# Attention over 32 steps on one core: rows' exponentials kept in every second step, exchanged in one pass

## The chip, the core and the metric

The kernel runs on one core of a Trainium2 chip. A core has a matmul engine (TensorE, PE in the profile, with its weight loads as PEld), VectorE (DVE), ScalarE (ACT), GpSimd (POOL), a queue engine that issues transfers (SyncE, SP) and 16 DMA engines. PE writes its results into PSUM, eight banks of 512 fp32 values on each of 128 partitions; everything else is in SBUF. The engines run beside one another and wait for each other on semaphores; each takes its own instructions in order. The metric is the device time of one execution in microseconds (us).

## The reference

```python
# x: (8, 512, 512) f32, cond: (8, 512); 16 heads of 32
Q, K, V   = split_heads(x @ Wq.T + bq), split_heads(x @ Wk.T + bk), split_heads(x @ Wv.T + bv)
tQ, tK    = split_heads(tokens @ Wq.T + bq), split_heads(tokens @ Wk.T + bk)   # tokens = cond[:, None, :]
scores    = einsum('bhqd,bhkd->bhqk', Q + tQ, K + tK) / sqrt(32)
attn      = softmax(scores, axis=-1)
out       = x + merge_heads(einsum('bhqk,bhkd->bhqd', attn, V))
```

All in fp32. There are 8 batches of 512 rows, and 16 heads.

## The kernel before, in words

The work is cut into T = 32 steps. Step t treats batch b = t // 4 and four heads (group g = t % 4), each head on 32 partitions or columns of a tile of 128.

A step needs, for each head, the scores with the queries on the partitions ("row scores", `row_scores`, L585: four blocks qc of 128 queries against 512 keys). VectorE takes their maxima (`one_max`, L552, or two heads at once in `row_max_of`, L594), ScalarE their exponentials with the row sums (`denominators`, L640). For the product with V, PE wants the exponentials with the keys on the partitions. There are two ways to get them.

In an ordinary step PE makes the scores a second time, transposed (`exponentials`): L692 puts the negated maximum into the bank, split into three bf16 parts, and L695 adds the scores; ScalarE writes the exponentials as tiles "e" (L706). The first exponentials are thrown away after their sums. The maxima reach L692 by `split_max` (four small operations, L654 to L657) and `turn_max` (a transposing DMA, L666).

In a step of the list `BLOCKED` (L71: 3, 7, ... 27, seven steps) the first exponentials are kept: `denominators` writes them to an SBUF tile of 32 KB a partition, VectorE transposes them in blocks of 32 x 32 (`turn_blocks`, L605, 8 units of 1024 columns), and SP's transfers exchange the blocks between the four groups of 32 partitions (`swap_blocks`, L624): for each half of the rows six pairs are swapped by three moves through two tiles from the pool of "e", 36 transfers of 128 KB a step. No second scores, maxima's split or transposes are made for such a step. `times_v` (L715) reads either kind.

Projections of x to Q, K and V are made for two groups of a batch at a time with seven products instead of eight (`product`, L441). `first_products` combines them on VectorE, `first_by_others` has ScalarE copy them and GpSimd add them, `other_products` does the second half on VectorE. `combine_x` and `combine_w` prepare sums of blocks on GpSimd.

The main loop (L1009) runs t from 1 to 28 with four items each. Every item has one row of scores (of step t + 1, the last one of step t + 2) and one piece of PE work: "q", "k" or "v" (a projection product for a later batch) or "V" (`weighted`: the product of step t − 1 with V, the sums spread by `spread_sums`, the reciprocal, and `send`). In a step that isn't kept, an item also makes a quarter of the step's second scores. `send` transposes the result on VectorE (L779), scales it and adds the residual x on GpSimd (L780, L781) and stores it with SP. `load_residual` (L188, L196) loads x and adds the bias on GpSimd. `turn_x` (L351) transposes the next batches' x on VectorE, and `load_block` (L170) loads it with SP. The eight PSUM banks are handed from item to item by `begin` and `released`.

The order of PE, ScalarE, VectorE and GpSimd is the order of the program text; SP's transfers are ordered by the scheduler. After the loop, steps 29 to 31 are finished by code of their own, with the tile "late" in the room of the kept rows.

Of the kernel before, what the change touches and what calls it, by code (L numbers as in the profile page):

```python
# [17 lines left out]
def kernel(  # L18
# [52 lines left out]
    BLOCKED = [t for t in range(3, T - 4, G)]  # L71
# [3 lines left out]
    xp = ctx.enter_context(tc.tile_pool(name="xp", bufs=3))  # L75
    xtp = ctx.enter_context(tc.tile_pool(name="xtp", bufs=2))
    qkp = ctx.enter_context(tc.tile_pool(name="qkp", bufs=3))
    ep = ctx.enter_context(tc.tile_pool(name="ep", bufs=10))
# [100 lines left out]
    def load_residual(t):  # L179

        b, g = divmod(t, G)
        if turned_by_vector(t):
            if late:
                xr[t] = late[0][:, 2, :].rearrange("p (f e) -> p f e", e=BL)
            else:
                xr[t] = op.tile([P, NB, BL], F32, tag="xr", name=f"xr_{t}")
            for h in range(HG):
                nc.sync.dma_start(  # L188
                    xr[t][h * BL : (h + 1) * BL], spread(x[b], g * P + h * BL)
                )  # L190
            bias = bvs[:, g, :].unsqueeze(1).broadcast_to([P, NB, BL])
        else:

            xr[t] = xT[b][:, g, :]
            bias = bvl.broadcast_to([P, S])
        nc.gpsimd.tensor_tensor(xr[t], xr[t], bias, ALU.add)  # L196

    EB = ctx.enter_context(tc.tile_pool(name="eb", bufs=1))

    def room(name):  # L200
        return EB.tile([P, HG, NS, HG, P], F32, tag="eb", name=name)

    early = room("early").rearrange("p g c h s -> p (g c) (h s)")
# [4 lines left out]
    def load_w(n, w, queue, cs=range(NC)):  # L208
        wv = w.rearrange("(c p) d -> p c d", p=P)
        for c in cs:  # L210
# [9 lines left out]
                mybir.EngineType.Pool,  # L220
            }
# [108 lines left out]
    def transpose_x(n, pt, leaves=nc.vector.tensor_copy):  # L330

        b, sc = divmod(n, NS)
        if b >= B:
            return
        if sc == 0:
            xT[b] = xtp.tile([P, NC, S], F32, tag="xT", name=f"xT_{b}")
        for cc in range(NC):
            nc.tensor.transpose(
                pt[:, cc * P : (cc + 1) * P], xs[n][:, cc * P : (cc + 1) * P], ident
            )  # L340
        leaves(xT[b][:, :, sc * P : (sc + 1) * P], pt.rearrange("p (c s) -> p c s", c=NC))
        if n:
            load_block(n + 3)

    def turn_x(n):
        b, cc = divmod(n, NC)
        if b >= B:
            return
        if cc == 0:
            xT[b] = xtp.tile([P, NC, S], F32, tag="xT", name=f"xT_{b}")  # L350
        nc.vector.transpose(xT[b][:, cc, :], xs[n].rearrange("p f i -> p (f i)"))  # L351
        to_load.append(n + 3)
# [136 lines left out]
    def first_by_others(n, b, u, dens, small, at):  # L489

        one_, two_ = banks(at), banks(at + 1)
        c1, c12, c2, c22 = parts_of(n, b, u)
        dens()
        product(n, b, u, 1, one_[:, :HS])
        product(n, b, u, 6, two_[:, HS:])
        small()
        product(n, b, u, 2, two_[:, :HS], (0,))
        product(n, b, u, 7, one_[:, HS:])
        m1 = c2[:, 0, :]
        nc.scalar.copy(m1, one_[:, :HS])  # L500
        if n == "v":
            nc.scalar.copy(c1[:, 0, :], two_[:, :HS])
            nc.scalar.copy(c12, two_[:, HS:])
            nc.scalar.copy(c22, one_[:, HS:])
        else:
            nc.scalar.copy(c1, halves(two_))
            add = tok[:, "qk".index(n), u * 2 + 1, b : b + 1]
            nc.scalar.activation(c22, one_[:, HS:], AF.Identity, bias=add)
        for o in (c1[:, 0, :], c12):
            nc.gpsimd.tensor_tensor(o, o, m1, ALU.add)  # L510
        nc.gpsimd.tensor_tensor(c22, c22, c12, ALU.add)
# [44 lines left out]
    def row_max(t, qc, hold=False, w=HG):  # L556
# [14 lines left out]
        def held():  # L571
            if apart or hold and t < T - 2:
                for j in range(2):
                    one_max(t, qc, 2 + j, last[j])
            else:
                row_max_of(t, qc, 1, both)
# [21 lines left out]
    blocked = {}  # L598

    def turn_blocks(t, units):  # L600

        for n in units:
            pr = slice(n % NP * 2, n % NP * 2 + 2)
            e = blocked[t][:, :, n // NP, pr, :].rearrange("p g h s -> p g (h s)")
            nc.vector.transpose(e, e)  # L605

    APART = [(a, g) for a in range(HG) for g in range(a + 1, HG)]
    between = {}

    def swap_blocks(t, half, move):  # L610

        def part(a, g):
            e = blocked[t][a * BL : (a + 1) * BL, g, half * 2 : half * 2 + 2]
            return e.rearrange("p c h s -> p (c h s)")

        if move == 0:
            between[t, half] = [
                ep.tile([P, 2, S], F32, tag="e", name=f"between_{t}_{half}_{i}") for i in range(2)
            ]
        for n, (a, g) in enumerate(APART):  # L620
            at = (n + 2) % HG * BL
            kept = between[t, half][n // HG][at : at + BL].rearrange("p i s -> p (i s)")
            to, of = [(kept, part(a, g)), (part(a, g), part(g, a)), (part(g, a), kept)][move]
            nc.sync.dma_start(to, of)  # L624

    def denominators(t, qc, w=HG):
# [3 lines left out]
        for j in range(HG):  # L630
            if t in BLOCKED:
                if t not in blocked:
                    blocked[t] = room(f"blocks_{t}")
                to = blocked[t][:, :, qc, j, :].rearrange("p g (c e) -> p g c e", e=BL)
            else:
                to = banks(w + j)
# [50 lines left out]
    def exponentials(t, kc, at=None):  # L687
# [5 lines left out]
        for j in range(HG):  # L693
# [7 lines left out]
            )  # L701
        for pr in range(NP):
            e = ep.tile([P, 2, S], F32, tag="e", name=f"e_{t}_{kc}_{pr}")
            es[t, kc, pr] = e
# [3 lines left out]
    def times_v(t, kc, pt, chunks=range(NS)):  # L708
        b, g = divmod(t, G)
        for j in range(HG):  # L710
            if t in BLOCKED:
                e = blocked[t][:, :, :, j, kc * BL : (kc + 1) * BL].rearrange("p a c e -> p c a e")
# [63 lines left out]
    def send(t, y_, rec):  # L776

        y = op.tile([P, NB, BL], F32, tag="res", name=f"res_{t}")
# [3 lines left out]
        b, g = divmod(t, G)  # L782
        for h in range(HG):
            nc.sync.dma_start(spread(out[b], g * P + h * BL), y[h * BL : (h + 1) * BL])  # L784
# [167 lines left out]
    load_residual(1)  # L952
# [19 lines left out]
    def products(t, n, blocks, hold, dens, small):  # L972

        b, r = (t - 1) // G + 1, (t - 1) % G
        if r % 2:
            hold()
            other_products(n, b, r // 2, dens, small, (0, 3))
            released(1, 2, 4, 5, 6, 7, 0, 3)
        elif blocks and n == "v":
            first_products(n, b, r // 2, dens, small, 5, 4, hold)  # L980
            released(6, 7, 0, 1, 2, 3, 5, 4)
        elif blocks:
            hold()
            first_by_others(n, b, r // 2, dens, small, 4)
            released(6, 7, 0, 1, 2, 3, 5, 4)
        else:
            first_products(n, b, r // 2, dens, small, 1, 0, hold)
            released(2, 3, 4, 5, 6, 7, 1, 0)

    TURNED = [((1, 1), (0, 1), (0, 1), (0, 1)), ((0, 0), (0, 1), (0, 1), (0, 1))]  # L990
    turned = {}

    def turn_more(t, i, late):

        for u in (t, t + 1):
            if u in BLOCKED:
                n = turned.get(u, 0)
                turned[u] = n + TURNED[t + 1 - u][i][late]
                turn_blocks(u, range(n, turned[u]))

    SWAPS = {
        (-1, 2): [(0, 0)],
        (-1, 3): [(0, 1), (0, 2)],
        (0, 3): [(1, 0)],
        (1, 0): [(1, 1)],
        (1, 1): [(1, 2)],
    }

    for t in range(1, T - 3):  # L1009
# [3 lines left out]
        items = ["q", "k", "v", "V"] if t - 1 in BLOCKED else ["V", "q", "k", "v"]  # L1013
        for i, item in enumerate(items):
# [4 lines left out]
            late_first = item in ("v" if blocks else "qkv") and t % 2 == 1  # L1019
            hold = row_max(*rows, late_first, w)  # L1020

            def held(i=i, hold=hold):
                hold()
                if i == 2:
                    split_max(t + 1)
                    turn_max(t + 1)

            dens = lambda: denominators(*rows, w)
            if item in "qkv":
                products(t, item, blocks, held, dens, nothing)  # L1030
            else:
                held()
                dens()
                if blocks:
                    weighted(t - 1, banks(4), banks(5), nothing)
                    released(6, 7, 0, 1, 2, 3, 5, 4)
                else:
                    weighted(t - 1, banks(0), banks(1), lambda: turn_more(t, i, 0))
                    released(2, 3, 1, 4, 5, 6, 7, 0)
            if i == 0 and r == 0:  # L1040
                turn_x(t + NC + 2)
                turn_x(t + NC + 3)
            if i == 0 and r == 1:
                combine_x(b + 1, 1, nc.gpsimd)
            if i == 1 and r == 0:
                combine_x(b + 1, 0, nc.gpsimd)
            if i == 2 and r == 1:
                turn_x(t + NC + 3)
                turn_x(t + NC + 4)
            if i == 3:  # L1050
# [3 lines left out]
            if i == 3:  # L1054
                load_residual(t + 1)
            turn_more(t, i, 1)
            for u in (t - 1, t, t + 1):
                if u in BLOCKED and (t - u, i) in SWAPS:
                    for swap in SWAPS[t - u, i]:
                        swap_blocks(u, *swap)  # L1060
# [26 lines left out]
    def crossed(t, kc, qc, u=None):  # L1087
# [27 lines left out]
        maxima((2, 3))  # L1115
        for pr in (1, 0):
            e = ep.tile([P, 2, S], F32, tag="e", name=f"e_{t}_{kc}_{pr}")
            es[t, kc, pr] = e
# [8 lines left out]
    late.append(room("late").rearrange("p g c h s -> p (g c) (h s)"))  # L1127
# [24 lines left out]
    load_residual(t)  # L1152
    load_residual(t + 1)
# [41 lines left out]
    y30 = op.tile([P, NB, BL], F32, tag="res", name=f"res_{t - 1}")  # L1195
# [83 lines left out]
```

## Time and profile before

| what | before |
|---|---|
| time, median of 3 runs | 691.5 us (691.21 to 692.53) |
| the profiled execution | 689.72 us, its span 687.9 us |
| PE, PEld busy | 677.3 us (98%), 311.7 us (45%) |
| VectorE, ScalarE, GpSimd busy | 563.3 us (82%), 563.7 us (82%), 233.3 us (34%) |
| moved by DMA | 65.50 MB, mean 95 GB/s |
| SP's queue (q1) | 63.05 MB, 47.4% of 16 engines |

The profile is of one execution, whose own time is 689.72 us. The span runs from the first to the last instruction. A line of the profile names a line of the kernel, the engine, the operation, the tile written and read, partitions x elements and the number of instructions. "Idle before" is time in which the engine waited just before such an instruction, with what ended the wait. In a timeline the columns are start, duration and group; matmuls overlap, so a group's time is read from start to start.

### The profile page before, as it was taken

How to read it: one execution, taken by the hardware profiler on the slowest of the kernel's cores; microseconds unless marked ns; L12 is line 12 of the kernel's file. 1: busy time of each engine (PE TensorE's matmuls, PEld its weight loads, DVE VectorE, ACT ScalarE, POOL GpSimd, SP SyncE). 2: the span in 40 equal slices, each digit the busy share in tenths (PEclk: the TensorE clock that was granted, in tenths of full speed). 3: DMA queues.
4: the chain of work that ended last, by engine and by line, in shares of the span. 5: the costliest groups of instructions: out<-in, count | busy, mean ns of one | idle time of the engine just before them, and what ended most of it. 6: DMA issues, size and time to landing. Idle time of an engine off the chain costs nothing.

```text
span 687.9 us, 22054 instructions
## 1 busy us (share of the span) xinstructions
PE 677.3 (98%) x8824; PEld 311.7 (45%) x8824; DVE 563.3 (82%) x878; ACT 563.7 (82%) x1427; POOL 233.3 (34%) x315
## 2 busy tenths in 40 slices
PE   9999999999999999999999999999999999999997
PEld 7444444444445444444444444453544544444332
DVE  4798799967989689886998778996798967987777
ACT  2589887988879898898888988798887989888664
POOL 3722412424233242424314252252423324241361
PEclk9999999999999999999999999999999999999999
DMA  6633235654376543663456624665427622376311
GB/s 183 104 54 60 40 64 133 129 106 70 52 155 143 90 71 78 132 155 61 68 118 122 143 49 77 135 125 113 72 40 154 148 54 41 66 135 151 53 31 31
DMA packets 231674, 65.50 MB, mean 95 GB/s; under 512 B 221834, under 2 KB 222346, under 8 KB 231572
## 3 DMA queue, kind: packets, MB, share of 16 engines
q1 hardware_dynamic: 229812, 63.05, 47.4%
q8 instruction: 69, 1.13, 0.7%
q10 hardware_dynamic: 1760, 1.05, 0.5%
q14 instruction: 33, 0.27, 0.1%
HBM read 19.75 MB, written 8.39 MB: 41 GB/s over the span
## 4 chain that ended last, share of the span: by engine, by line
PE 88%; DMA 3%; POOL 3%; SPq 2%; ACT 1%; DVE 1%; issue 1%; DVEq 0%; POOLq 0%; ACTq 0%
PE psum L441 37%; PE psum L715 16%; PE psum L585 16%; PE psum L695 11%; PE psum L692 4%; PE psum L384 2%; DMA maxT<-split 2%; SPq L784 1%; ACT psum L640 1%; SPq L188 1%; DMA xr<-in_x_dram 1%; POOL res L781 1%; DMA w_q<-in_L_cond_Wq_dram 1%; DVE nmax L552 1%; PE psum L725 1%
## 5 line engine op out<-in xcount | busy, mean ns | idle before, releaser
L640 ACT ACTIVATE psum<-psum,nmax 128x512 f32<-128x512 f32 x368 | 244.7, 673 | 29.0 <-DVE nmax L552 21.2
L552 DVE TENSOR_REDUCE nmax<-psum 128x1 f32<-128x512 f32 x298 | 191.3, 683 | 79.6 <-PE psum L585 77.2
L706 ACT ACTIVATE e<-psum 128x512 f32<-128x512 f32 x376 | 194.2, 602 | 61.2 <-PE psum L695 57.7
L585 PE MATMUL psum<-kT,qT 32*128 32x512 f32 x1024 | 143.0, 605 | 0.0
L594 DVE TENSOR_REDUCE nmax<-psum 128x2 f32<-128x1024 f32 x101 | 122.5, 1214 | 1.3 <-PE psum L585 1.3
L695 PE MATMUL psum<-qT,kT 32*128 32x512 f32 x752 | 96.7, 587 | 0.0
L715 PE MATMUL psum<-e,v 128*32 128x512 f32 x800 | 95.3, 597 | 0.0
L780 POOL TENSOR_TENSOR res<-res,recs 128x512 f32<-128x512 f32 x30 | 31.4, 1048 | 172.4 <-DVE res L779 172.4
L196 POOL TENSOR_TENSOR xr<-xr,bvs 128x512 f32<-128x512 f32 x30 | 38.4, 1280 | 141.8 <-DMA xr<-in_x_dram 141.8
L585 PEld LDWEIGHTS psum<-kT,qT 32*128 32x128 f32 x1024 | 60.9, 182 | 52.7 <-issue 22.0
L640 ACT ACTIVATION_READ_ACCUMULATOR psum<-psum,nmax 128x1 f32 x368 | 78.7, 214 | 0.0
L640 ACT ACTIVATE blocks<-psum,nmax 128x512 f32<-128x512 f32 x112 | 76.2, 719 | 0.0
L605 DVE STREAM_TRANSPOSE blocks<-blocks 128x1024 f32<-128x1024 f32 x56 | 68.5, 1223 | 0.0
L441 PE MATMUL psum<-wc_v,xc 128*32 128x256 f32 x768 | 50.2, 379 | 0.0
L441 PE MATMUL psum<-xc,wc_q 128*32 128x256 f32 x720 | 47.1, 379 | 0.0
L441 PE MATMUL psum<-xc,wc_k 128*32 128x256 f32 x720 | 47.1, 379 | 0.0
L715 PEld LDWEIGHTS psum<-e,v 128*32 128x32 f32 x800 | 20.8, 110 | 51.4 <-issue 29.2
L692 PE MATMUL psum<-maxT,onesb 3*128 3x512 bf16 x376 | 37.1, 385 | 3.0 <-DMA maxT<-split 2.3
L781 POOL TENSOR_TENSOR res<-res,xr 128x512 f32<-128x512 f32 x30 | 38.5, 1282 | 2.4
L695 PEld LDWEIGHTS psum<-qT,kT 32*128 32x128 f32 x752 | 37.4, 185 | 1.7
L441 PE MATMUL psum<-wT_v,xT 128*32 128x256 f32 x512 | 36.8, 382 | 0.0
L779 DVE STREAM_TRANSPOSE res<-psum 128x512 f32<-128x512 f32 x28 | 20.1, 717 | 18.4 <-PE psum L715 15.4
(179 smaller groups left out, 862.9 us busy)
## 6 DMA issues: line engine op xcount, KB each, us to landing
between<-blocks SPq DMA_DIRECT2D x84, 128.0 KB, 2.4
blocks<-blocks SPq DMA_DIRECT2D x84, 128.0 KB, 2.3
blocks<-between SPq DMA_DIRECT2D x84, 128.0 KB, 2.4
out_dram<-res SPq DMA_DIRECT2D x122, 64.0 KB, 1.9
xr<-in_x_dram SPq DMA_DIRECT2D x120, 64.0 KB, 2.4
x<-in_x_dram SPq DMA_DIRECT2D x112, 64.0 KB, 2.4
w_q<-in_L_cond_Wq_dram SPq DMA_DIRECT2D x4, 256.0 KB, 4.2
w_v<-in_L_cond_Wv_dram SPq DMA_DIRECT2D x16, 64.0 KB, 2.3
```

What stands on the lines that cost most here:

```text
L196: nc.gpsimd.tensor_tensor(xr[t], xr[t], bias, ALU.add)
L441: nc.tensor.matmul(pt[r], still[:, r], moving, start=(kc == kcs[0]), stop=(kc == kcs[-1]))
L552: nc.vector.tensor_reduce(nmax[t][:, qc, j : j + 1, 0], pt, AX.X, ALU.max, negate=True)
L585: nc.tensor.matmul(pt, qkT["q", t][r, qc * P : (qc + 1) * P], qkT["k", t][r, :], start=True, stop=True,)
L594: nc.vector.tensor_reduce(nmax[t][:, qc, pr * 2 : pr * 2 + 2, 0], pt, AX.X, ALU.max, negate=True)
L605: nc.vector.transpose(e, e)
L640: nc.scalar.activation(to, of, AF.Exp, bias=nmax[t][:, qc, j, :], accum_out=sums[t][:, qc, j, :],)
L692: nc.tensor.matmul(bank[j], onesb[r, :], maxT[t][r, :], start=True, stop=False)
L695: nc.tensor.matmul(bank[j], qkT["k", t][r, kc * P : (kc + 1) * P], qkT["q", t][r, :], start=False, stop=True,)
L706: nc.scalar.activation(e[:, i, :], bank[pr * 2 + i], AF.Exp)
L715: nc.tensor.matmul(pt[j * HD : (j + 1) * HD, :], vs[b % 2][:, kc, (g * HG + j) * HD : (g * HG + j + 1) * HD], e, start=(kc == chunks[0]), ...
L781: nc.gpsimd.tensor_tensor(y, y, xr.pop(t), ALU.add)
```

## The change

- `BLOCKED` holds every second step, 3, 5, ... 27: thirteen steps.
- The kept rows have one tile "kept" for the whole kernel. The "e" tiles become a ring "e" of six chunks of 8 KB a partition; the first four are also the target of the exchange (`crossed_over`), and an ordinary step writes its four chunks in turn, starting behind the four.
- `cross_over` replaces `swap_blocks`: 16 transfers, also those of a block to its own partitions, from "kept" to the ring, three quarters of the rows (192 KB each) in the first item of the kept step and the last quarter (64 KB each) in its third. They are issued by SP and by GpSimd, as `QUEUES` says.
- SP's order is written out too. Stores are issued in the last item of a step, residuals are loaded in the last item for the step itself.
- Kept steps have the items "V", "q", "k", "v", others "q", "V", "k", "v". Kept steps make all three first products by ScalarE and GpSimd. Maxima are split on VectorE. Maxima in kept steps are taken one by one. The block transposes, 5 in the step before and 3 in the kept step, and the transposes of x are called between the parts of an item.
- Two buffers of x instead of three, one for the residual and one for the result instead of two.

```diff
-    BLOCKED = [t for t in range(3, T - 4, G)]
+    BLOCKED = [t for t in range(3, T - 4, 2)]
-    xp = ctx.enter_context(tc.tile_pool(name="xp", bufs=3))
+    xp = ctx.enter_context(tc.tile_pool(name="xp", bufs=2))
-    ep = ctx.enter_context(tc.tile_pool(name="ep", bufs=10))
...
-                xr[t] = op.tile([P, NB, BL], F32, tag="xr", name=f"xr_{t}")
+                xr[t] = op.tile([P, NB, BL], F32, tag="xr", name=f"xr_{t}", bufs=1)
...
+    rows_kept = const.tile([P, HG, NS, HG, P], F32, tag="kept", name="kept")
+
+    NK = 6
+    E = const.tile([P, NK, NP, 2, S], F32, tag="e", name="e")
+    crossed_over = E[:, :NS].rearrange("p k r i s -> p (k r i s)")
+    crossed_over = crossed_over.rearrange("p (a c h s) -> p a c h s", a=HG, c=NS, h=HG)
+    chunk = [NS - 1]
+
+    def chunk_of():
+        chunk[0] = (chunk[0] + 1) % NK
+        return E[:, chunk[0]]
...
                 mybir.EngineType.Pool,
+                mybir.EngineType.SP,
...
     def first_by_others(n, b, u, dens, small, at, between):
...
+        if n == "v":
+            between()
         nc.scalar.copy(m1, one_[:, :HS])
         if n == "v":
             nc.scalar.copy(c1[:, 0, :], two_[:, :HS])
             nc.scalar.copy(c12, two_[:, HS:])
-            nc.scalar.copy(c22, one_[:, HS:])
+            nc.vector.tensor_copy(c22, one_[:, HS:])
         else:
...
+            between()
...
-            if apart or hold and t < T - 2:
+            if apart or w == 0 or hold and t < T - 2:
...
+    def cross_over(t, qcs, queues):
+
+        for n in range(HG * HG):
+            i, a = divmod(n, HG)
+            g = (a + i) % HG
+            queues[n].dma_start(
+                crossed_over[g * BL : (g + 1) * BL, a, qcs].rearrange("p c h s -> p (c h s)"),
+                rows_kept[a * BL : (a + 1) * BL, g, qcs].rearrange("p c h s -> p (c h s)"),
+            )
+        chunk[0] = NS - 1
...
-                e = blocked[t][:, :, :, j, kc * BL : (kc + 1) * BL].rearrange("p a c e -> p c a e")
+                e = crossed_over[:, :, :, j, kc * BL : (kc + 1) * BL].rearrange("p a c e -> p c a e")
...
-        y = op.tile([P, NB, BL], F32, tag="res", name=f"res_{t}")
+        if late:
+            y = late_part(13 + t % 2).rearrange("p (f e) -> p f e", e=BL)
+        else:
+            y = op.tile([P, NB, BL], F32, tag="res", name=f"res_{t}", bufs=1)
...
+        to_store.append((t, y))
+        if row_of[0] is None:
+            store()
...
+    TURNED = [(1, 1, 1, 1), (1, 1, 1, 0)]
     turned = {}
-
-    def turn_more(t, i, late):
+    S_, G_ = nc.sync, nc.gpsimd
+    QUEUES = {
+        0: (slice(0, 3), [S_, S_, G_, S_, S_, S_, G_, G_] * 2),
+        2: (slice(3, 4), [S_, G_] * 8),
+    }
+
+    def turn_more(t, i, more=0):
 
         for u in (t, t + 1):
             if u in BLOCKED:
                 n = turned.get(u, 0)
+                turned[u] = n + (more or TURNED[t + 1 - u][i])
                 turn_blocks(u, range(n, turned[u]))
+        if t in BLOCKED and i in QUEUES:
+            cross_over(t, *QUEUES[i])
...
-        items = ["q", "k", "v", "V"] if t - 1 in BLOCKED else ["V", "q", "k", "v"]
+        items = ["V", "q", "k", "v"] if blocks else ["q", "V", "k", "v"]
...
-                    split_max(t + 1)
+                    split_max(t + 1, nc.vector if blocks else nc.gpsimd)
                     turn_max(t + 1)
...
+            def between(i=i):
+                turn_more(t, i)
+                if i == 3 and t % 2:
+                    turn_x(t + 7)
+                    turn_x(t + 8)
+
+            if i == 0 and r == 1:
+                combine_x(b + 1, 1, nc.gpsimd)
...
-                    weighted(t - 1, banks(0), banks(1), lambda: turn_more(t, i, 0))
+                    weighted(t - 1, banks(0), banks(1), between)
+                    turn_more(t, i, 1)
...
             if i == 3:
-                load_residual(t + 1)
+                store()
+                load_residual(t)
```

## The prediction

> **What bounds the kernel now.** I read the page's busy line and its chain first, then the timeline of the matmul engine inside one step, then windows cut to whole steps, then the DMA queue's timeline.
>
> ```profile
> PE 677.3 (98%) x8824; PEld 311.7 (45%) x8824; DVE 563.3 (82%) x878; ACT 563.7 (82%) x1427; POOL 233.3 (34%) x315
> ...
> PE 88%; DMA 3%; POOL 3%; SPq 2%; ACT 1%; DVE 1%; issue 1%; DVEq 0%; POOLq 0%; ACTq 0%
> ```
>
> PE is busy for 98% of the span, and the chain that ended last is 88% PE. Since a busy PE need not be a fast one, the timeline decides. These are two "k" items: the first in step 10, which has no kept rows, the second in step 11, which has (start, duration, group).
>
> ```profile
> 262.73 0.39 PE L692 MATMUL psum<-maxT,onesb 3*128 3x512 bf16 x4
> 262.96 1.03 PE L695 MATMUL psum<-qT,kT 32*128 32x512 f32 x8
> 263.82 1.03 PE L585 MATMUL psum<-kT,qT 32*128 32x512 f32 x8
> 264.78 1.07 PE L441 MATMUL psum<-xc,wT_k 128*32 128x256 f32 x16
> ...
> 267.94 0.40 PE L692 MATMUL psum<-maxT,onesb 3*128 3x512 bf16 x4
> ...
> 282.20 1.14 PE L585 MATMUL psum<-kT,qT 32*128 32x512 f32 x8
> 283.27 1.07 PE L441 MATMUL psum<-xT,wT_k 128*32 128x256 f32 x16
> ...
> 286.43 1.14 PE L585 MATMUL psum<-kT,qT 32*128 32x512 f32 x8
> ```
>
> No line has an idle mark: groups follow one another. The first item lasts 267.94 − 262.73 = 5.21 us, the second 286.43 − 282.20 = 4.23 us, since it has no second scores (L692, L695). Windows that begin and end with the row scores of a step show all engines (busy us and instructions of PE, PEld, DVE, ACT, POOL; then clock, DMA share, GB/s): steps 8 and 9, steps 10 and 11, 9, 10 and 11 alone, and a stretch of the DMA exchange.
>
> ```profile
> 210.33:252.94 42.61, 42.61 (x581) 20.11 (x576) 33.39 (x57) 38.08 (x96) 15.94 (x21) 1.00 0.56 107
> 252.94:291.75 38.81, 38.81 (x533) 17.19 (x530) 35.41 (x50) 32.76 (x86) 11.70 (x17) 1.00 0.50 100
> 231.64:252.94 21.30, 21.30 (x293) 10.22 (x290) 16.05 (x31) 18.98 (x48) 10.72 (x13) 1.00 0.43 71
> 252.94:273.26 20.32, 20.32 (x280) 8.99 (x274) 18.95 (x26) 18.19 (x46) 3.87 (x4) 1.00 0.35 63
> 273.26:291.75 18.49, 18.49 (x257) 8.20 (x256) 16.46 (x25) 14.57 (x42) 7.83 (x13) 1.00 0.67 142
> ...
> 278.70:282.40 3.70, 3.70 (x64) 1.92 (x64) 3.45 (x5) 2.66 (x9) 2.33 (x2) 1.00 0.92 210
> ```
>
> The clock is full throughout and PE fills every step. A pair of steps without kept rows takes 42.61 us, a pair with one such step 38.81 us. After the change steps 3 to 28 are thirteen such pairs; now there are seven.
>
> **The change, part by part.**
>
> *Second scores removed (gain).* Six more steps lose four groups each of L692, L695 and the exponentials of L706. The price is read from whole pairs, which hold the neighbours' work too: 42.61 − 38.81 = 3.80 us, times 6 = 22.8 us. ACT loses 16 × 602 ns per step and takes over copies; in the pair with kept rows it is busy 32.76 of 38.81 us, so it isn't the bound.
>
> *More block transposes and moved products (VectorE).* Each new step adds 8 transposes of 1223 ns. From the pair 10 and 11: 35.41 us, minus the v products that go to ACT and POOL (four operations, starting 0.33 us apart: 1.3), plus one copy (0.33), the split of the maxima that comes from POOL (four operations; the four that DVE does at the kernel's end take 0.71, 0.18, 0.20 and 0.23: 1.3), two x transposes that this pair lacks now (1.29 for two) and single maxima where pairs were (about 0.2): 37.2 of 38.81 us, 96%. In step 10, with DVE at 18.95 of 20.32, PE already lost 0.1 us at the row scores of 269.03 (1.14 us, not 1.03). In the new "k" item maxima, split and transpose are 2.4 + 1.3 + 1.15 = 4.9 us against an item of 4.23, and the "v" item behind it has 0.3 us to spare, so a delay reaches the next row. ACT's copies of the "v" products, about 0.8 us, now end after the next row scores want their banks. The bounds for both are 0 and 1.0 us a pair (the excess 0.7 plus half the copies); I take 0.3, since the surplus of "q" and "V" takes up most of it: 13 × 0.3 = 3.9 us.
>
> *One-pass exchange.* 36 transfers of 128 KB become 16 of 192 KB (three quarters of the rows) and 16 of 64 KB. Now each set of six has 3.7 us of SP issue and moves on the DMA engines like this:
>
> ```profile
> between<-blocks SPq DMA_DIRECT2D x84, 128.0 KB, 2.4
> blocks<-blocks SPq DMA_DIRECT2D x84, 128.0 KB, 2.3
> ...
> 278.70 3.79 SPq L624 DMA_DIRECT2D blocks<-between  x6
> ```
>
> Two deadlines are new. Call S0, S1, S2, S3 the starts of the four items of a kept step (4.71, 4.23, 4.23, 4.23 us apart).
>
> First, the 3.15 MB of the first set start when the "V" item's matmuls have read the ring chunks and DVE has turned the sixth unit, about S1 + 0.3. ACT writes row 0 of the step after next into the same kept tile in the last item, at about S3 + 2.0 (in step 11: row scores 286.43, ACT 288.44). That is 10.2 us after the start; a transfer now has 1.25 us before its first packet and 0.35 after its last, by the trace's packets, so 8.6 us remain for the data: 366 GB/s. What lies queued behind ACT's wait is the whole row, the "v" copies, and PE two groups later, so lateness passes to PE at nearly full size, in 12 steps (step 29 keeps no rows). The rate is not in the trace for two queues. Below, the SP queue alone: 210 GB/s at a share of 0.92 is 228 at full share, 13.8 us, 5.2 us late. Above, the shortest 4 KB packets (156 ns against a mean of 283) on 16 engines: 420 GB/s, 7.5 us, not late. I take 350 (9.0 us, 0.44 late, 12 × 0.44 = 5.3 us), nearer to the fast end, because reads are split between lower and upper partitions by queue (POOL's six all read from the upper 64, eight of SP's ten from the lower), while every transfer now is followed by another of the same queue.
>
> A rule of the Trainium skill speaks against this: "DMA: Bandwidth & Descriptors", rules for kernel authors, says that spreading DMAs over queues saves only issue time, since all share 16 engines; by it the rate would stay 228 and the kernel would end near 735. "SBUF — State Buffer", on the DMA port swizzle, says that 32 partitions reach half of the ports and partitions 64 apart lie on different ones; by it two transfers in different halves could go at twice the rate and the term would be 0. No row before the change shows either.
>
> Second, POOL issues DMAs for the first time, 6 and 8 per kept step. Its price has no row. Below: SP's plain issue, 0.62 us; above: SP's transposing issue, 1.21 us (L666). With g for one issue, POOL has 6g, the previous result's two operations (2.3), the "q" additions (2.2), then 8g, and a landing of 2.3 from the last issue. The "V" item of the next step wants all of it at S2 + 15.7. Counting from S1 + 0.3 this is 13g − 12.8 us late: nothing up to g = 0.99, 2.9 at 1.21. I take 0.8, nearer to the plain issue, as the transfers are plain: nothing. POOL's busy time in a pair would then be about 11.7 + 11 (14 issues) + 2.2 (v additions) + 2.6 − 1.0, some 27 of 39 us.
>
> *SP in written order.* SP issues in a pair 18 exchange transfers, 8 loads of x, 8 residual loads, 8 stores at 0.5 to 0.62 us and one transpose of 1.2: about 25 of 39 us. Stores and residual loads stand behind the exchange, and the result and the residual have one buffer each now: VectorE's next result transpose waits for the store. The store of an odd step would land about S2 + 14.4, the transpose that follows comes at S2 + 19.4: 5 us to spare, so nothing, unless the exchange holds SP up that long. If the exchange backs up, the transposed maxima (issued in the "k" item, wanted 4 us later) are late as well; that belongs to the first rival. Fewer x buffers (2, not 3) still leave four items between load and use. Start and end of the kernel stay as they are: 0, bounds −1 and +2 us (chain shares SPq 2% and DMA 3% lie there).
>
> Sum: 689.7 us is the profiled execution (span 687.9 and 1.8 around it), 1.8 below the median of 691.5; I carry the difference to the median: 691.5 − 22.8 + 3.9 + 5.3 = 677.9, say 678 us.
>
> **Rivals.**
>
> *The exchange holds ACT (slower).* Place: ACT's kept-row write in the last item of a kept step. It decides from (22.8 − 3.9)/12 = 1.58 us lateness, which is 10.1 us of data or 310 GB/s; the digits of the page speak for it, as no slice moves over 183 GB/s. Against it: POOL's transfers are on the other half. At 228 GB/s: 691.5 − 22.8 + 3.9 + 62 = 735; at 290 (10.8 us, 2.3 late) 700.
>
> *POOL's queue makes the second set late (slower).* From g = 1.1 us; at 1.21: 691.5 − 22.8 + 3.9 + 13 × 2.9 = 710 without any other lateness. For it: POOL waits in order, and the "q" additions stand between the two sets. Against it: the page has POOL at 34%.
>
> *DVE sets the pace (less gain).* If each pair loses the full 1.0 us and the exchange as taken: 691.5 − 22.8 + 13 + 5.3 = 687.
>
> *It isn't faster because stalls eat just the gain:* within 0.2%, 690 to 693.
>
> **How the numbers follow.** 0.2% (1.4 us) is about what a measurement of this kernel can tell from no change. Forecast as summed, 668 to 684: 0.46. DVE pace, or exchange late by 1 to 1.5 us, 684 to 690: 0.16. Within 0.2%: 0.04. Exchange holds ACT: 0.23, about half of it above 712. POOL: 0.11, 693 to 712. Faster 0.62, same 0.04, slower 0.34. Below 668 would need a gain over 3.8 us a step: 0.03; above 712 some 0.14; so the range is 668 to 712, and the forecast's own 668 to 684.
>
> **What would show it.** Right: pairs of about 39 to 40 us between row scores, no L692 and L695 in odd steps, PE still over 95%, DVE about 95%, ACT's kept-row exponentials (L640) without a wait on a DMA. Wrong: "ACT kept <- DMA" among the longest waits with PE idle in the item behind it; PE waiting for the exchange before L715; POOL issues over 1.0 us each; DMA share in the exchange near 0.9 at 230 GB/s, not 350.

## The result: 15% slower, and the profile after

The changed kernel takes 797.57 us (median of 4 runs, 795.61 to 799.92), the kernel before beside it 692.01 us. The ratio is 1.152, 95% interval [1.147, 1.157]. The forecast was 678 us, the range ended at 712. The profiled execution took 796.48 us with a span of 794.7 us, 1.1 us below the median.

The page of the changed kernel: busy time, granted clock and the chain of waits.

```profile
PE 689.5 (87%) x8536; PEld 307.0 (39%) x8536; DVE 610.5 (77%) x918; ACT 541.8 (68%) x1406; POOL 357.9 (45%) x496
...
PEclk9999997997989979899897998979989899998999
...
PE 70%; DMA 11%; DVE 9%; SPq 7%; issue 2%; ACT 1%; POOL 0%; DVEq 0%; ACTq 0%
```

PE has 288 matmuls fewer than before and yet is busy for 12 us longer: the clock digits fall to 7 at places, where before the clock was full throughout. PE's share of the chain fell from 88% to 70%; DMA and SP's queue now hold 18%. Which transfers they are stands in the longest waits (engine, line and tile that waited, what it waited for: total us, times, longest).

```profile
PEld L691 <- DMA maxT<-split: 103.2, 13, 9.6
ACT kept L639 <- DMA e<-kept: 96.7, 11, 10.4
...
PE psum L691 <- DMA maxT<-split: 82.0, 11, 9.1
```

There are two waits, both in the last item of a kept step. ScalarE waits to write kept rows until the exchange has read them, which the forecast named as a rival. PE waits nearly as long for the transposed maxima "maxT" at L691, which it named only as a by-product of that rival. One pair of steps (15 and 16) in timelines: first PE, start, duration, group and idle time before it.

```profile
421.35 1.05 PE L448 MATMUL psum<-wc_v,xc 128*32 128x256 f32 x16
430.33 1.58 PE L691 MATMUL psum<-maxT,onesb 3*128 3x512 bf16 x4 [7.93 <-DMA maxT<-split]
431.33 2.28 PE L694 MATMUL psum<-qT,kT 32*128 32x512 f32 x8
433.20 2.35 PE L595 MATMUL psum<-kT,qT 32*128 32x512 f32 x8
...
439.32 1.03 PE L694 MATMUL psum<-qT,kT 32*128 32x512 f32 x8
440.18 1.05 PE L595 MATMUL psum<-kT,qT 32*128 32x512 f32 x8
```

ScalarE in the same item:

```profile
419.15 0.52 ACT L517 ACTIVATE kT<-psum,tok 128x256 f32<-128x256 f32 x1
429.83 0.69 ACT L639 ACTIVATE kept<-psum,nmax 128x512 f32<-128x512 f32 x1 [10.16 <-DMA maxT<-split]
```

And SP's queue:

```profile
410.76 13.67 SPq L621 DMA_DIRECT2D e<-kept  x10
424.53 2.48 SPq L665 DMA_TRANSPOSE maxT<-split  x1
427.11 5.13 SPq L621 DMA_DIRECT2D e<-kept  x8
```

PE stands still for 7.93 us and ScalarE for 10.16, side by side. The releaser printed for ScalarE is the maxima's transfer, which was merely the last to end; ScalarE's instruction writes "kept" and needs the exchange to have read it. SP needed 13.67 us to issue ten transfers, and the transposing DMA behind them left at 424.53. After the stall PE's groups take about twice their normal time, 2.28 and 2.35 us against 1.03 and 1.05 a few items later.

Windows of the same pair of steps (busy us and instructions of PE, PEld, DVE, ACT, POOL; clock, DMA share, GB/s): the whole pair, the stretch in which the first set moves, two pieces of the stall and the restart, and an undisturbed piece behind.

```profile
404.93:455.32 50.39, 42.37 (x533) 18.53 (x529) 38.30 (x57) 33.55 (x91) 23.36 (x33) 0.90 0.57 119
...
411.90:428.40 16.50, 10.50 (x168) 5.01 (x160) 11.74 (x19) 7.75 (x22) 13.14 (x22) 0.93 0.97 229
424.00:427.00 3.00, 0.00 (x0) 0.00 (x0) 0.08 (x1) 0.00 (x0) 2.90 (x6) 0.87 1.01 242
427.00:430.30 3.30, 0.00 (x0) 0.00 (x0) 0.00 (x0) 0.47 (x1) 0.52 (x2) 0.50 0.88 145
430.30:433.20 2.90, 2.78 (x12) 1.52 (x14) 0.29 (x1) 2.90 (x11) 0.00 (x0) 0.50 0.47 114
433.20:436.80 3.60, 3.60 (x28) 1.47 (x26) 1.79 (x4) 3.22 (x8) 2.13 (x3) 0.55 0.63 106
436.80:439.00 2.20, 2.20 (x44) 1.08 (x36) 1.73 (x3) 1.92 (x6) 0.37 (x1) 1.00 0.71 112
```

The pair takes 50.39 us; the forecast's pair was 38.81 + 0.3 us, plus 0.44 us of lateness. While the first set moves, the DMA engines are full (share 0.97) at 229 GB/s with all their traffic; the forecast had 350. The granted clock falls to 0.50 while PE idles and stays there for some us behind.

Over all 13 pairs, read from the starts of the row scores, the last item of a kept step takes 14.10 us on average, and the item behind it 6.58.

### The profile page after: what moved, and what is told of

It reads as the page before. It is cut to its first block, busy times and chain, and to the rows that moved or that the text cites. A ratio compares the mean times of both kernels' runs of the same rounds, so it can differ in the third digit from the quotient of the medians.

```text
span 794.7 us, 21892 instructions
## 1 busy us (share of the span) xinstructions
PE 689.5 (87%) x8536; PEld 307.0 (39%) x8536; DVE 610.5 (77%) x918; ACT 541.8 (68%) x1406; POOL 357.9 (45%) x496
## 3 DMA queue, kind: packets, MB, share of 16 engines
q10 hardware_dynamic: 1760, 1.05, 0.5%
## 4 chain that ended last, share of the span: by engine, by line
PE 70%; DMA 11%; DVE 9%; SPq 7%; issue 2%; ACT 1%; POOL 0%; DVEq 0%; ACTq 0%
PE psum L448 25%; PE psum L595 14%; PE psum L714 14%; PE psum L694 9%; DMA maxT<-split 8%; SPq L621 6%; DVE nmax L562 5%; PE psum L691 3%; DMA e<-kept 2%; PE psum L391 2%; DVE kept L614 1%; DVE rest L654 1%; ACT psum L639 1%; DVE split L653 1%; ACT kept L639 1%
## 5 line engine op out<-in xcount | busy, mean ns | idle before, releaser
L562 DVE TENSOR_REDUCE nmax<-psum 128x1 f32<-128x512 f32 x352 | 220.5, 678 | 54.0 <-PE psum L595 52.2
L639 ACT ACTIVATE kept<-psum,nmax 128x512 f32<-128x512 f32 x208 | 141.6, 693 | 114.5 <-DMA e<-kept 96.7
L639 ACT ACTIVATE psum<-psum,nmax 128x512 f32<-128x512 f32 x272 | 180.2, 666 | 48.7 <-DVE nmax L562 47.3
L705 ACT ACTIVATE e<-psum 128x512 f32<-128x512 f32 x280 | 144.6, 602 | 54.5 <-PE psum L694 52.1
L595 PE MATMUL psum<-kT,qT 32*128 32x512 f32 x1024 | 160.5, 665 | 0.0
L621 POOL DMA_DIRECT2D e<-kept x182 | 90.3, 503 | 82.9 <-DVE res L781 34.4
L614 DVE STREAM_TRANSPOSE kept<-kept 128x1024 f32<-128x1024 f32 x104 | 126.7, 1218 | 0.0
L714 PE MATMUL psum<-e,v 128*32 128x512 f32 x1024 | 121.2, 596 | 0.0
L691 PE MATMUL psum<-maxT,onesb 3*128 3x512 bf16 x280 | 34.0, 424 | 97.5 <-DMA maxT<-split 82.0
L604 DVE TENSOR_REDUCE nmax<-psum 128x2 f32<-128x1024 f32 x74 | 89.8, 1215 | 1.3 <-PE psum L595 1.3
L595 PEld LDWEIGHTS psum<-kT,qT 32*128 32x128 f32 x1024 | 60.6, 196 | 66.3 <-issue 24.4
L691 PEld LDWEIGHTS <-onesb 3*128 3x128 bf16 x280 | 7.3, 92 | 136.3 <-DMA maxT<-split 103.2
L639 ACT ACTIVATION_READ_ACCUMULATOR psum<-psum,nmax 128x1 f32 x272 | 56.7, 208 | 0.0
L639 ACT ACTIVATION_READ_ACCUMULATOR kept<-psum,nmax 128x1 f32 x208 | 43.5, 209 | 0.0
```

The lines of the kernel that those rows point to most:

```text
L562: nc.vector.tensor_reduce(nmax[t][:, qc, j : j + 1, 0], pt, AX.X, ALU.max, negate=True)
L595: nc.tensor.matmul(pt, qkT["q", t][r, qc * P : (qc + 1) * P], qkT["k", t][r, :], start=True, stop=True,)
L604: nc.vector.tensor_reduce(nmax[t][:, qc, pr * 2 : pr * 2 + 2, 0], pt, AX.X, ALU.max, negate=True)
L621: queues[n].dma_start(crossed_over[g * BL : (g + 1) * BL, a, qcs].rearrange("p c h s -> p (c h s)"), rows_kept[a * BL : (a + 1) * BL, g, q ...
L639: nc.scalar.activation(to, of, AF.Exp, bias=nmax[t][:, qc, j, :], accum_out=sums[t][:, qc, j, :],)
L691: nc.tensor.matmul(bank[j], onesb[r, :], maxT[t][r, :], start=True, stop=False)
```

## The experiments

Kernels without a range or an interval were executed once. The kernel before took 691.7 to 694.1 us beside them.

**Rate of the exchange alone.** No part of the computation is made; bursts of block moves follow one another, each after the one before has landed.

```diff
+    def two_as_kernel():
+        queues = [S_, S_, G_, S_, S_, S_, G_, G_] * 2
+        for n in range(16):
+            i, a = divmod(n, 4)
+            move(queues[n], a, (a + i) % 4, a)
+    def sp_low_pool_high():
+        for j in range(4):
+            move(S_, 0, 1, j)
+            move(G_, 2, 3, j)
```

> Leaves out the whole computation: it moves blocks between groups of 32 partitions in nine kinds of burst, each twice, one burst after the other, and copies x to the output. Theory 1 (all transfers between groups of 32 partitions share what limits one queue, about 225 GB/s, whatever the queues and groups): 16 x 192 KB take 13 to 14.5 us of data with SP alone and with SP and POOL as in the changed kernel; 8 x 192 KB take 6.5 to 7.5 us in every mixture. Theory 2 (lower and upper 64 partitions are separate, and two queues use both; what the forecast leaned on): SP alone inside the lower half 6.9 us, SP in the lower beside POOL in the upper half 3.6 to 4.5 us, the kernel's mixture 8 to 10 us.

Windows cut to the data of eight bursts, all moves of 192 KB unless said. Columns: window, length, VectorE, GpSimd, clock, DMA share, GB/s. In order: the kernel's 16 moves on SP; the same on SP and GpSimd as in the kernel; SP, lower 64 partitions only; SP, lower and upper in turn; SP lower beside GpSimd upper; SP lower beside GpSimd lower; SP lower beside ScalarE upper; two moves of 128 partitions on SP.

```profile
19.25:33.23 13.98, 0.00 (x0) 0.00 (x0) 1.00 0.99 225
51.65:65.45 13.80, 0.00 (x0) 2.14 (x5) 1.00 0.96 228
84.35:92.07 7.72, 0.00 (x0) 0.00 (x0) 1.00 0.96 203
104.75:111.27 6.52, 0.00 (x0) 0.00 (x0) 1.00 0.96 241
140.90:147.76 6.86, 0.00 (x0) 1.03 (x3) 1.00 0.88 229
158.59:166.72 8.13, 0.00 (x0) 1.03 (x3) 1.00 0.91 193
178.41:184.78 6.37, 0.00 (x0) 0.00 (x0) 1.00 0.98 247
196.01:199.97 3.96, 0.00 (x0) 0.00 (x0) 1.00 0.97 396
```

One queue or two makes no difference (225 against 228). Which halves are in flight together matters by 28% at most (193 to 247). Only a move over all 128 partitions went much faster, at 396 GB/s (330 in its repetition, whose end ran beside the copy to the output); the exchange as it is written has no such moves, and moves over 64 or 96 partitions were not tried. The forecast's 350 GB/s doesn't exist for this set; its lower bound, 228, is the rate.

**Half of the bytes.** Of each set only the last 8 of the 16 transfers are made.

```diff
             i, a = divmod(n, HG)
+            if i < 2:
+                continue
...
```

> The changed kernel with 8 of the 16 transfers of each set left out (those to the own group and to the next one), so half of what step t's V product reads is stale. Theory 1 (bytes at 225 GB/s): the first set takes 7 us, is read before ACT writes the kept tile again, and SP comes to the maxima in time: 672 to 700 us, clock 0.98 or more. If the stall comes from the order of the queues and the waits and not from bytes: 770 us or more.

It takes 676.88 us, beside 692.69 of the kernel before. A pair in the windows (columns as above):

```profile
366.38:405.59 39.21, 39.21 (x533) 17.41 (x528) 37.13 (x57) 33.15 (x89) 22.50 (x28) 1.00 0.48 99
```

PE fills the whole pair and the clock is full. ScalarE's wait for the exchange is 4.6 us in the whole kernel, PE's matmuls wait 0.5 us for the maxima. The other parts of the change are in this kernel: the order of items, the moved products, the single buffers, half of GpSimd's issues. So what makes the change slow, 120.7 us (797.57 − 676.88), hangs on the exchange, and the rest does about what was forecast. The items account for that: (14.10 − 5.39) + (6.58 − 5.85) = 9.44 us a pair between the two traces, times 13 is 122.7. Half of the transfers are also half of the issues, so this run alone doesn't part the bytes from the issues. (The last kernel below moves all the bytes, in 48 transfers a step instead of 32, without the stall.)

**One wait at a time.** ScalarE's wait is taken away by leaving row 0 of kept steps in its bank, so that this quarter of the rows isn't kept; PE's by handing the transposing DMA to ScalarE's queue, behind ScalarE's copies of the "k" item, or by making the transposition of the maxima on PE, with a copy by VectorE.

```diff
(row0_psum)
-            if t in BLOCKED:
+            if t in BLOCKED and qc:
...
(maxt_act)
-        nc.sync.dma_start_transpose(
+        nc.scalar.dma_start_transpose(
...
(pe_max)
-                    turn_max(t + 1)
+                    if not blocks:
+                        turn_max(t + 1)
...
+                if blocks and i == 3:
+                    small = lambda: transpose_max(t + 1, banks(6))
...
```

> The changed kernel, but the first row of every kept step is thrown into its bank, as in ordinary steps, so ACT never waits for the exchange to have read it; that row's exponentials are left out of the kept tile. Theory 1: the maxima are still late behind the exchange, 770 to 800 us, with the wait moved from ACT to PE before the second scores. Theory 4 (ACT's write into the kept tile alone): 675 to 690 us.

> The changed kernel with the transposing DMA of the maxima issued by ScalarE's queue behind its copies, not by SP behind the exchange. Theory 1 (the exchange's data rate holds both ACT's kept-row write and the maxima; either is enough to stop PE): little gain, 775 to 800 us, ACT still waits 8 to 10 us a pair for the exchange. Theory 3 (SP's written order alone: the maxima stand behind ten issues): the pair loses about 9 us, 670 to 690 us.

> Both edits: the maxima on ScalarE's queue and the first row not kept (left out). Theory 1: the stall at the end of the kept step goes; what stays is the second set of the exchange, which 4 MB at 225 GB/s bring about 1 us after the next V item wants it: 672 to 695 us, clock back at 0.99 or more. Theories 3 and 4: the same time as the one of the two single edits that they name, 670 to 690.

> The changed kernel with the maxima transposed by four matmuls and a copy in the v item of the kept step, all rows kept and sent. Only ACT's wait for the kept tile is left. Theory 1: either wait alone is enough, so little is gained: 765 to 795 us, ACT waits for the exchange 7 to 10 us a pair. If the maxima alone had held PE: 680 to 715 us.

> The changed kernel with the maxima transposed by four matmuls and a copy in the v item of the kept step (no DMA for them), and the first row of kept steps thrown away (left out of the kept tile), so neither of the two waits on DMA at that place is left. Theory 1: the exchange is as slow as before, but only the next V product waits for it, about 1 us a pair: 676 to 700 us, clock 0.98 or more. If something else holds the kept step's end (VectorE or GpSimd): above 720.

| kernel | us | waits that are left in kept steps |
|---|---|---|
| changed kernel | 797.57 | ScalarE 96.7 us, PE 82.0 us |
| row 0 not kept | 794.27 | PE for the maxima 101.5 us, 13 times |
| maxima through ScalarE's queue | 823.22 | ScalarE for the exchange 132.6 us, 12 times; PE for the maxima 70.9 us, 13 times |
| both of these | 775.27 | PE for the maxima 73.0 us, 13 times; ScalarE for the exchange 2.2 us |
| maxima turned on PE, all rows kept | 792.77 | ScalarE for the exchange 109.7 us, 12 times |
| maxima turned on PE, row 0 not kept | 712.63 | ScalarE for the exchange 23.7 us, 10 times, one row later; the last item of a kept step takes 6.1 to 8.5 us, the "q" item behind it 5.8 to 9.5 |

Either wait alone is enough: taking away the one leaves the time within 5 us of 797.57, since the other ends at nearly the same time. Without both the kernel is 80 to 82 us below those with one of them left. That excludes a story with only one of the two. The lines of the two kernels with one wait left and of the one with neither at row 0:

```profile
PE psum L691 <- DMA maxT<-split: 101.5, 13, 9.3
ACT kept L639 <- DMA e<-kept: 109.7, 12, 10.0
ACT kept L639 <- DMA e<-kept: 23.7, 10, 4.0
```

The last of them is a part of why 712.63 us is still above the kernel with half of the bytes: the exchange is late for the next kept row too, in the "q" item. Three expectations were missed here: 823.22 us is above 775 to 800, 775.27 far above 672 to 695, and 712.63 above 676 to 700. Handed to ScalarE's queue, the maxima make it worse by 26 us: both waits stay, and ScalarE's grows from 96.7 to 132.6 us.

The kernel with both edits tells why the maxima stay late off SP's queue. Its DMA issues (queue, count, median us to landing):

```profile
maxT<-split ACTq DMA_TRANSPOSE x16, 7.7
```

ScalarE's queue and PE there:

```profile
411.29 1.77 ACTq L665 DMA_TRANSPOSE maxT<-split  x1
```

```profile
418.99 0.61 PE L691 MATMUL psum<-maxT,onesb 3*128 3x512 bf16 x4 [4.70 <-DMA maxT<-split]
```

In this pair the transfer is issued right behind ScalarE's copies at 411.29 and its maxima can be used at 418.99. Before the change the same transfer landed in 2.5 us. So SP's order isn't the whole of it: issued amid the exchange, the small transfer itself takes three times as long. That is what the expectation for both edits had left out.

**The new exchange, but in seven steps only.**

```diff
-    BLOCKED = [t for t in range(3, T - 4, 2)]
+    BLOCKED = [t for t in range(3, T - 4, G)]
```

> The changed kernel with kept rows in seven steps as before (3, 7, ... 27), but with the new exchange, queues and order. Theory 1: each kept step still pays its stall of about 10 us, with the next kept row four steps away (ACT need not wait there, the maxima must): 730 to 765 us. If the thirteen steps' total of transfers is the trouble (the DMA engines full on average): 688 to 700.

It takes 759.07 us, 66.4 above the kernel before beside it (692.69), with the same number of kept steps. Put on the exchanges alone, that is 9.5 us for each of the seven. With thirteen, 797.57 minus the forecast's sum without the exchange (691.5 − 22.8 + 3.9 = 672.6) is 125, or 9.6 a step. So the price is one of each exchange, not of their number. With seven kept steps the new exchange, with what came with it, is worse than the old one; the old one was not run with thirteen. No wait of ScalarE is put down to the exchange here, as the next kept row is four steps away. The maxima alone make the stall:

```profile
PE psum L691 <- DMA maxT<-split: 50.0, 7, 7.4
```

The last item of a kept step takes 13.2 to 13.9 us.

**An earlier and evener exchange.** All that is computed in the kernel is computed here. The exchange is cut into four sets: for rows 0 and 1, the blocks out of the upper two groups of 32 partitions start one item earlier, on GpSimd's queue, those of the lower two in the kept step's first item on SP's; row 2 follows on both queues, and row 3 in the third item as before. An ordinary step starts its chunks at another place of the ring, so that the early blocks find their target free. PE turns the maxima as above. Stores and loads of the residual stand ahead of the last set.

```diff
-    chunk = [NS - 1]
+    chunk = [1]
...
-    QUEUES = {
-        0: (slice(0, 3), [S_, S_, G_, S_, S_, S_, G_, G_] * 2),
-        2: (slice(3, 4), [S_, G_] * 8),
+    SETS = {
+        (-1, 3): [(slice(0, 2), (2, 3), [G_])],
+        (0, 0): [(slice(0, 2), (0, 1), [S_]), (slice(2, 3), (0, 1, 2, 3), [S_, G_])],
+        (0, 2): [(slice(3, 4), (0, 1, 2, 3), [S_, G_])],
     }
...
```

> All rows kept and sent, all outputs computed. The maxima by four matmuls and a copy; the exchange in four sets: rows 0 and 1 of the blocks that go to ring chunks 2 and 3 in the last item of the step before, the rest of rows 0 and 1 first in the kept step, then row 2, then row 3; a kept step's store and residual load stand before the last set. Theory 1: the same bytes at the same rate, but 1 MB moved ahead of the window and ACT's rows freed first: no stall of over 1 us a pair, 672 to 692 us, clock 0.99 or more. If the exchange needs more than the window whatever its order: 710 or more.

It takes 719.78 us, ratio 1.038 [1.031, 1.045]. That lies where the rival was expected (710 or more), not theory 1; the two kernels that follow are faster with the same bytes. No wait of ScalarE is put down to the exchange any more, and PE's waits are short. Two of them, the exchange's last set (7.2 us in all, in the "V" item, where SP issues stores and loads ahead of that set) and VectorE's copy of the maxima, stand like this:

```profile
PE psum L695 <- DVE maxT L685: 15.1, 13, 2.0
...
PE psum L718 <- DMA e<-kept: 7.2, 4, 2.5
```

The "V" item takes 5.7 to 9.9 us, the last item of a kept step 6.7 to 9.5. So the next kernel puts the stores behind the last set, gives the split to GpSimd ahead of the additions of "q", and has ScalarE copy the maxima:

```diff
-                    split_max(t + 1, nc.vector if blocks else nc.gpsimd)
+                    split_max(t + 1)
+                    while added:
+                        added.pop(0)()
...
+                    small = lambda: transpose_max(t + 1, banks(6), nc.scalar.copy)
...
```

> As early, all outputs computed, with three of its left waits taken out: store and residual load behind the last set again (they held SP's share of it 4.5 us), the split of the maxima on GpSimd before the q additions (VectorE's took up to 0.8 us an operation beside GpSimd), and ScalarE copies the transposed maxima before its row's exponentials. Theory 1: V items back at 5.7 to 6.2 us, the item behind a kept step at 5.3 to 6 us, 680 to 700 us. If the total of transfers at 225 GB/s is too much for a pair: 710 to 725 as early.

It takes 699.06 us, ratio 1.0069 [1.004, 1.010]: nearly the kernel before. Pairs are regular, the last item 6.52 us and the next 6.49 in nearly all. What is left stands in its waits:

```profile
ACT maxT L691 <- PE psum L685: 25.1, 14, 2.6
```

ScalarE waits 1.8 us a pair for PE's transposes, ahead of its exponentials. The last kernel gives this copy to VectorE, which the split has left free, and has ScalarE make the denominators first again:

```diff
     def first_by_others(n, b, u, dens, small, at, between):
+        dens()
         product(n, b, u, 1, one_[:, :HS])
         product(n, b, u, 6, two_[:, HS:])
         small()
-        dens()
...
-                    small = lambda: transpose_max(t + 1, banks(6), nc.scalar.copy)
+                    small = lambda: transpose_max(t + 1, banks(6), nc.vector.tensor_copy)
```

> The exchange in four sets begun early, as in the run before, but the turned maxima are copied out of their bank by VectorE behind TensorE's four transposes, and ScalarE does the denominators first again, so that no ScalarE instruction waits for the transposes. Nothing is left out. Theory (bytes no longer hold anything; what the run before lost is ScalarE's wait of about 1.9 us a pair for the transposes): that wait goes, the last item of a kept step takes 5.3 to 5.7 us and the next one 5.3 to 6.0, a pair about 39.5 us, and the kernel 676 to 688 us, below the kernel before. Rival (the items are long for TensorE's and VectorE's own work in the items around the hand-over, whoever copies): 695 to 702, with the wait moved to VectorE's copy or to TensorE's second scores.

It takes 678.48 us (675.04 to 683.75, 4 runs), beside 691.69 of the kernel before: ratio 0.982 [0.976, 0.988]. It is faster than the kernel before, by 1.2 to 2.4%; whether by 2% is not decided. The busy line of its page, and a pair of its steps in the windows:

```profile
PE 663.8 (98%) x8588; PEld 297.7 (44%) x8588; DVE 592.9 (88%) x879; ACT 540.7 (80%) x1406; POOL 431.4 (64%) x678
```

```profile
347.79:387.25 39.46, 39.46 (x537) 17.29 (x533) 36.93 (x54) 33.45 (x91) 29.25 (x48) 1.00 0.63 140
```

PE in the last item of a kept step:

```profile
363.89 0.40 PE L685 MATMUL psum<-identb,split 128*128 128x128 bf16 x4
364.22 0.64 PE L448 MATMUL psum<-wT_v,xT 128*32 128x256 f32 x8
364.67 1.05 PE L448 MATMUL psum<-wc_v,xc 128*32 128x256 f32 x16
365.65 0.40 PE L701 MATMUL psum<-maxT,onesb 3*128 3x512 bf16 x4
```

PE is without a gap again and the clock is full, though all 16 blocks of each step (4.19 MB) are exchanged. So neither the bytes nor the number of transfers are too many for a pair of steps; in the changed kernel they were moved too late or too close together. The hand-over of the maxima was reworked on the way as well, which brought 719.78 us down to 678.48. How much of the gain is the earlier start's and how much that of the maxima's way off the DMA engines was not tried one by one in this form: the kernel with the maxima on PE alone stood at 792.77 us, and the early exchange was run only together with it.

## Why the prediction was wrong

*Second scores removed, 22.8 us: right.* A kept step takes 18.49 us in the kernel with half of the bytes (18.49 in step 11 before), and PE fills the pair.

*VectorE and ScalarE, 3.9 us: size about half.* The pair of 39.21 us has VectorE busy for 37.13; the forecast had 37.2. The excess stands in the item behind a kept step, 5.85 us on average where most took 5.2 before; which of the two engines holds PE there was not parted. One reading was wrong: the 1.14 us at 269.03 are no loss to VectorE. All row scores without second scores ahead of them take 1.14, those at 282.20 and 286.43 too, and the item from 269.03 lasts 4.23 us like its neighbours. Averaged over the 13 pairs the items of that kernel add up to 39.53 us, 0.7 above 38.81 instead of 0.3, and inside the bounds 0 to 1.0. With 0.7 the sum without an exchange is 677.8, and 676.88 was measured.

*One-pass exchange, 5.3 us: the step that failed.* The place was right: the data must be read by the time ScalarE writes row 0 again. (9.0 − 8.6 is 0.4, not 0.44, which matters little.) The rate was wrong: "I take 350 ... nearer to the fast end, because reads are split between lower and upper partitions by queue". The bursts give 228 GB/s for exactly this set on these queues, the lower bound. That the halves are split by queue is worth 229 against 193 GB/s, not a doubling. The prediction weighed two rules of the Trainium skill, and the one that it followed was read too far. "DMA: Bandwidth & Descriptors", rules for kernel authors, was borne out by the bursts: a second queue brings nothing (225 on one, 228 on two). "SBUF — State Buffer", port swizzle, says which partitions share a port; a later heading of that page, "Can I just issue two DMAs to hit both halves?", answers its question with no. The bursts agree that nothing doubles: both halves at once reach 229 to 247 GB/s, beside 193 to 203 for the lower half alone.

*The price at 228 GB/s was too low as well.* The rival's 5.2 us of lateness and 735 us assume the first set alone on the engines. Four things came on top, and the term is 9.44 us a pair instead of 5.2 (13 × 9.44 = 122.7):

- The first set starts later than taken: SP's first transfer leaves 1.1 us behind S1 in every pair (410.76 here, S1 at 409.64), when VectorE's block transpose has ended, not 0.3. So some 7.8 us remain instead of 8.6.
- GpSimd's part of the second set goes in among the first: it is issued from 421.07, while the first set is still moving, and 3.67 MB of exchange move between 412 and 428.5 us, at 222 GB/s.
- The transposed maxima are late. SP's plain issues "at 0.5 to 0.62 us" were taken as fixed, though the trace before had some of up to 1.92; in this pair one takes 1.37 us on average (13.67 us for ten), so the transposing DMA leaves 13.8 us behind the first of them, and its landing rises from 2.5 to 6.0 us in the median. The step that costed SP's order at nothing, "unless the exchange holds SP up that long", and gave the late maxima no price of their own ("that belongs to the first rival") failed here too; the kernel without row 0 (794.27 us) and the one with seven kept steps show that this wait alone costs about the same.
- After a stall the clock is half for some us. From L691 at 430.33 to L595 it takes 2.87 us instead of the 1.09 of an item later, and the next item 6.98 instead of 5.85: about 2.9 us in this pair. The windows show the half clock; no run tells it apart from waits of these groups for ScalarE, so the size is an estimate from this one pair, and an upper one.

*GpSimd's issues, nothing: right.* Its issue takes 503 ns, below the lower bound 0.62. That rival falls.

*The rival "the exchange holds ACT", 0.23:* right about the place and the sign, wrong about the price, 735 at most, against 797.57. *DVE sets the pace:* its excess is inside the edges above. The range ended at 712 because half of this rival's chance was left above it, and even its full price was worked out for one wait, without the neighbours of that wait.

The prediction's own signs told it rightly: an "ACT kept <- DMA" among the longest waits, PE idle in the item behind it, and a DMA share near 0.9 at 230 GB/s.

## What to carry to other kernels

The rate of a set of transfers is read from what that form of transfer has reached in the trace, here 32 partitions to 32 partitions at 225 GB/s; a second queue isn't a reason to take more. While a burst filled the DMA engines, the small transfer of the maxima was late in the burst's queue (6.0 us) and in another (7.7), so list all that lands in such a stretch and ask who waits for it. Before shrinking a burst, look at when its first data is ready: the same bytes, a part of them begun an item earlier, with the small transfer taken off the DMA engines and its hand-over reworked, turned a ratio of 1.152 into 0.982.

## What the hardware showed that was not expected

- SP's issue of a plain transfer of 192 KB took up to 2.75 us (median of all 234 issues of the exchange 0.59), while GpSimd's took 0.49 to 0.66 throughout. Before the change the median of SP's exchange issues was 0.59 as well, the longest 1.92.
- A transposing DMA took 2.5 us from issue to landing before, 6.0 in the changed kernel and 7.7 on ScalarE's queue in the kernel with both edits (medians).
- The clock: PE's last group before the stall ends at about 422.4 us and the next begins at 430.33. The granted clock is 0.87 in the window from 424.00, 0.50 in those from 427.00 to 433.20, 0.55 in the next and full from 436.80: half the clock from about 426.2 to 436.4 us, if each window is taken as a mix of full and half. "TensorE: Matmul & The Clock Gate" of the Trainium skill, Part 1, puts half the clock after at least one idle window of about 3.4 us and full clock after at least one such busy one. The trace has about 4 us from the idle start to the fall and about 6 from the restart to the rise, which is longer than one such window.
- Two moves over 128 partitions together went at 396 GB/s, at 330 when repeated, the same bytes in moves of 32 partitions at 193 to 247.
